# Edge keys by rows behind tile 2's ReLUs, and more warm transposes, in a graph attention layer

## The chip, the cores and the metric

The kernel runs on one core of one Trainium2 chip. The metric is the device time of one execution in microseconds (us). The time before is 299.84 us, the median of three runs (299.47 to 299.85).

## What is computed

The layer takes 384 nodes with 1024 features, a list of 6528 edges (`src`, `dst` and a type each), and weights. It normalises, applies a ReLU, projects twice to queries, keys and values for 16 heads of 64, adds a mask that is built from the edges, takes a softmax, multiplies by the values, projects once more and adds the input:

```
h = maximum(layernorm(x), 0)
q = h @ wq.T + bq;  k = h @ wk.T + bk;  v = h @ wv.T + bv
q2 = (q @ wiq.T + biq) by heads;  k2, v2 likewise
mask = full((N, N), -inf);  mask[src, dst] = softplus(edge_type_weights)[edge_type - 1]
mask's diagonal: softplus(w)[3] where still -inf
attn = softmax(q2 @ k2^T * scale + mask)
out = x + (attn @ v2) @ wo.T + bo
```

An edge can stand in the list more than once; the last one counts. So the kernel has to find, for each edge, whether the same (src, dst) cell comes again later.

## The kernel before, in words

All matrices are float32, and each product is made of three TensorE products: every operand is split into a high part in a reduced float32 format and the low rest, and high x high, high x low and low x high are added (`mm3`, lines 368 to 370).

The weights come as 56 chunks of 128 x 1024 (512 KB), in the order v, q, iv, k, then iq and ik in turn, then o. `load(w)` issues the DMA of chunk w on SP's queue into one of four `raw` buffers, so load(4) waits until chunk 0 has been read for the last time, load(5) for chunk 1, and so on. `split_hi(w)` (L77, ScalarE) and `split_lo(w)` (L82, VectorE or GpSimd) make the two parts. `slot_head(w)`, called ahead of each chunk's products, splits chunk w + 2, evacuates the products of the slot before, and issues load(w + 5).

The start, where the change lies, treats the three tiles of 128 nodes (t = 0, 1, 2) one after another:

- `ln_bn` (L247) and `ln_mean` (L250) take the mean and variance of a tile on VectorE.
- `ln_sub` subtracts the mean. For tiles 0 and 1, ScalarE does columns 0 to 511 (L276) and GpSimd the rest (L278); for tile 2 VectorE does both halves (L280).
- `ln_transpose` turns the tile with eight TensorE transposes (L288), four to a PSUM bank.
- `ln_hi` is the ReLU, which also makes the high part (L295 on ScalarE, L297 on VectorE, for the first half of tile 2). `ln_lo` (L302, VectorE) makes the low part.
- `ln_root`, `ln_rstd` and `ln_row` make the row of reciprocal deviations by which the projections are multiplied afterwards (`evac_row`, L389 to L391).
- `warm(n)` (L308) issues n transposes of the identity whose results nobody reads. `WARM` says how many stand ahead of tile 0's transposes, after them, and after tile 1's.

Chunk 0 is split by VectorE (L344) and GpSimd (L346) in two halves. The products of chunks 0 and 1 are issued in pieces (`pieces`, L380), in the order in which their operands become ready; from chunk 2 on a chunk is 24 products (L368 to L370).

The mask is prepared beside this. Each edge gets a key, 384 src + dst. `key_rows` computes the keys in another layout on VectorE (L180) and stores them in DRAM (`krow`, L181). `key_load(g, s)` (L201) reads a stretch of them back, broadcast to all 128 partitions; key_load(0, 0), (0, 1) and (0, 2) bring what the first 18 chunks of edges need. `mask_detect` (L213, VectorE) compares each chunk of edges with its row; the first three stand behind the evacuation of chunk 0's products, and all three key loads are needed for them. `mask_index` (L219, L220) makes the addresses, GpSimd scatters the values into three tables in DRAM (L224), which SP has cleared (`table_clear`, L145), and `mask_load` (L233) and `mask_select` (L237) bring them back well behind.

The order on every engine is the order in which the program is written: nothing is rescheduled. A DMA on SP's queue that waits holds up all those written after it. The small loads (`erows`, `edges`, `bcol`, `etw`) and chunks 0 and 1 are issued on SP right after the three tiles of x.

Of the kernel before, what the change touches and what calls it, by code (L numbers as in the profile page):

```python
# [14 lines left out]
N, D, NT, KT, NP = 384, 1024, 3, 8, 8  # L15
# [7 lines left out]
def gnn_kernel(ctx: ExitStack, tc: tile.TileContext, x, edges, erows, etw, wq, wk, wv, wiq, wik, wiv, wo,  # L23
# [6 lines left out]
    nc = tc.nc  # L30
# [8 lines left out]
    EB = 6  # L39
    NTAB, RNG = 3, EC // 3  # L40
    JI = [0, 1, 3, 5, 8, 11, 14, RNG]
    WARM = (20, 3, 0)

    def bank(tag):
        return psum.tile([128, 512], F32, tag=tag, name=tag, bufs={"g": 3, "a": 1}.get(tag, 2))
# [14 lines left out]
    def load(w):  # L60
        if w >= NCH:
            return
        n, m = chunks[w]
        raw[w] = wpool.tile([128, D], F32, tag="raw", name="raw", bufs=4)
        nc.sync.dma_start(raw[w], W[n][m])

    def split_hi(w, dst=None, dve=False):
        if w >= NCH:
            return
        if dst is None:  # L70
            t = wpool.tile([128, 2, D], F32R, tag="whl", name="whl", bufs=4)
            dst = (t[:, 0, :], t[:, 1, :])
        whl[w] = dst
        if dve:
            nc.vector.tensor_copy(dst[0], raw[w])
        else:
            nc.scalar.activation(dst[0], raw[w], AF.Copy)  # L77
# [51 lines left out]
    def mask_consts():  # L129
        nc.gpsimd.memset(upper, 1.0)  # L130
        nc.gpsimd.affine_select(upper, upper, pattern=[[1, 128]], compare_op=OP.is_gt, fill=0.0, base=0,
                                channel_multiplier=-1)
        nc.gpsimd.iota(dump.bitcast(I32), pattern=[[0, 1]], base=CELLS, channel_multiplier=1)
        nc.gpsimd.tensor_copy(w8[:, 8:9], dump.bitcast(I32))
        nc.gpsimd.memset(zero, 0.0)
# [42 lines left out]
    def key_rows():  # L178

        nc.vector.scalar_tensor_tensor(krt[:, :EC], er[:, :EC], float(N), er[:, EC:], op0=OP.mult, op1=OP.add)  # L180
        nc.sync.dma_start(krow.rearrange("c j -> (c j)").rearrange("(p e) -> p e", p=128), krt[:, :EC])  # L181
# [5 lines left out]
    def parts(g):  # L187
        return [(r * RNG + g * PA, min(r * RNG + (g + 1) * PA, (r + 1) * RNG)) for r in range(NTAB)]
# [3 lines left out]
    def key_load(g, s):  # L192

        if s == 0:
            t = work.tile([128, 2, NT, N], F32R, tag="pt", name="rows")
            krv[g] = t.bitcast(F32).rearrange("p a k n -> p (a k n)")
        c0, c1 = parts(g)[s]
        dst = krv[g][:, s * PA * 128:(s * PA + c1 - c0) * 128]
        for c in range(c0, c1):
            rows[c] = krv[g][:, (s * PA + c - c0) * 128:(s * PA + c - c0 + 1) * 128]  # L200
        nc.sync.dma_start(dst, krow[c0:c1, :].rearrange("c j -> (c j)").partition_broadcast(128))  # L201
# [44 lines left out]
    def ln_bn(t, h):  # L246
        nc.vector.bn_stats(lnt[:, 30 + 12 * t + 6 * h:36 + 12 * t + 6 * h], xt[t][:, h * 512:(h + 1) * 512])  # L247

    def ln_mean(t):
        nc.vector.bn_aggr(lnt[:, 2 * t:2 * t + 2],  # L250
                          lnt[:, 30 + 12 * t:42 + 12 * t].rearrange("p (a b) -> p a b", a=2))
        if t < 2:
            nc.scalar.mul(negm[:, t:t + 1], lnt[:, 2 * t:2 * t + 1], -1.0)

    def ln_root():
        nc.scalar.activation(root, var, AF.Sqrt, bias=epsc, scale=0.25)
        nc.scalar.activation(vq, var, AF.Identity, bias=epsc, scale=0.25)
# [15 lines left out]
    def ln_sub(t, c0, c1, eng):  # L273
        src, dst = xt[t][:, c0:c1], xn[t][:, c0:c1]
        if eng is nc.scalar:
            nc.scalar.activation(dst, src, AF.Identity, bias=negm[:, t:t + 1])  # L276
        elif eng is nc.gpsimd:
            nc.gpsimd.tensor_tensor(dst, src, lnt[:, 2 * t:2 * t + 1].to_broadcast([128, c1 - c0]), OP.subtract)  # L278
        else:
            nc.vector.tensor_scalar(dst, src, lnt[:, 2 * t:2 * t + 1], None, op0=OP.subtract)  # L280

    def ln_transpose(t):
        pss = []
        for half in range(2):
            ps = bank("st"[half] if t < 2 else "ga"[half])
            for j in range(4):
                k = half * 4 + j
                nc.tensor.transpose(ps[:, j * 128:(j + 1) * 128], xn[t][:, k * 128:(k + 1) * 128], ident)  # L288
            pss.append(ps)
        return pss  # L290

    def ln_hi(t, half, ps, eng=None):
        hi = hT[:, 0, half * 4:half * 4 + 4, t * 128:(t + 1) * 128]
        if eng is None:
            nc.scalar.activation(hi, ps.rearrange("p (k n) -> p k n", k=4), AF.Relu)  # L295
        else:
            eng.tensor_scalar(hi, ps.rearrange("p (k n) -> p k n", k=4), 0.0, None, op0=OP.max)  # L297
# [7 lines left out]
    def warm(n):  # L305
        for i in range(n):
            ps = bank("g")
            nc.tensor.transpose(ps[:, :128], ident, ident)  # L308

    mask_consts()  # L310
    warm(WARM[0])
    ln_bn(0, 0)
# [4 lines left out]
    p0 = ln_transpose(0)  # L317
    warm(WARM[1])
    ln_bn(1, 0)
# [6 lines left out]
    ln_bn(2, 0)  # L326
    ln_bn(2, 1)
    ln_mean(2)
    key_rows()
    load(2)  # L330
    load(3)
    for s in range(NTAB):
        key_load(0, s)
    ln_sub(2, 0, 512, nc.vector)
    ln_sub(2, 512, D, nc.vector)
    p1 = ln_transpose(1)
    warm(WARM[2])
    ln_hi(1, 0, p1[0])
# [8 lines left out]
    load(4)  # L347
    ln_hi(2, 0, p2[0], nc.vector)
    ln_hi(2, 1, p2[1])
    split_hi(1)  # L350
    ln_root()
    ln_lo(0, 0, p0[0])
# [533 lines left out]
```

## Time and profile before

| | |
|---|---|
| median of the three runs | 299.84 us |
| the profiled execution's own time | 298.95 us |
| its span, first to last instruction | 297.2 us |
| TensorE busy | 291.2 us, 98% of the span |
| VectorE, ScalarE, GpSimd busy | 202.4, 153.8, 155.7 us |
| first product of the projections | 10.16 us from the span's start |

The profile is that of one execution. PE is TensorE, PEld its loads of stationary operands, DVE VectorE, ACT ScalarE, POOL GpSimd, SP the engine whose queue issues most DMAs. A row of the timeline gives the start and the duration in us, the engine, the line of the code, the operation, what it writes and reads, its shape and how many were merged; in brackets stands the engine's idle time before it and what ended that. A merged row starts with the first of its instructions and ends with the last. TensorE's instructions overlap, so the time that each takes up is the distance from one start to the next, less than the duration shown. A row of the chain gives start, length and what was on the path that ended last.

### The profile page before, as it was taken

The page shows a single profiled execution, that of the slowest core. Times are in us where ns is not written, and L with a number is a line of the kernel's source. Part 1 is how long each engine was busy: PE and PEld are TensorE (multiplying, and loading weights), DVE is VectorE, ACT ScalarE, POOL GpSimd, SP SyncE. Part 2 cuts the span into 40 slices and gives each one's busy share as a digit, 9 for nine tenths or more (in the row PEclk, how much of TensorE's full clock was granted, in tenths as well). Part 3 has the DMA queues.
Part 4 walks back from the last instruction along what each step waited for, and adds up shares of the span by engine and source line. Part 5 has one row for each costly group of instructions (what it writes and reads, how often), then busy time and mean ns, then how long its engine had stood idle before and what let it go on. Part 6 is the DMA issues. An engine that isn't in the chain of part 4 may idle for free.

```text
span 297.2 us, 4982 instructions
## 1 busy us (share of the span) xinstructions
PE 291.2 (98%) x1654; PEld 276.5 (93%) x1654; DVE 202.4 (68%) x495; ACT 153.8 (52%) x288; POOL 155.7 (52%) x160
## 2 busy tenths in 40 slices
PE   6999999999999999999999999999999999999995
PEld 5999999999988889999999999999999998888884
DVE  4958977766856553888865676868686766696423
ACT  3784644433422222554336677778777767865310
POOL 3774567363857785710033656373746467976210
PEclk9999999999999999999999999999999999999999
DMA  7899864645396648393369784738374656900005
GB/s 279 277 324 398 292 207 131 225 143 212 116 303 202 197 153 289 113 342 112 117 167 261 206 216 115 202 93 223 99 221 121 170 144 176 348 10 0 2 3 209
DMA packets 22377, 55.12 MB, mean 185 GB/s; under 512 B 4816, under 2 KB 8400, under 8 KB 22352
## 3 DMA queue, kind: packets, MB, share of 16 engines
q1 hardware_dynamic: 19968, 52.42, 56.0%
q0 software_dynamic: 2064, 1.80, 2.1%
q10 hardware_dynamic: 320, 0.59, 0.9%
q8 instruction: 13, 0.21, 0.3%
q14 instruction: 12, 0.10, 0.1%
HBM read 40.39 MB, written 4.97 MB: 153 GB/s over the span
## 4 chain that ended last, share of the span: by engine, by line
PE 96%; DVE 1%; DMA 1%; ACT 0%; issue 0%
PE g L370 21%; PE g L368 21%; PE g L369 21%; PE a L758 6%; PE s L721 6%; PE t L741 5%; PE g L380 3%; PE s L369 2%; PE s L370 2%; PE s L368 2%; PE t L370 2%; PE t L369 2%; PE t L368 2%; DMA g<-in_x_dram 1%; DVE lnt L247 1%; PE a L369 1%
## 5 line engine op out<-in xcount | busy, mean ns | idle before, releaser
L368 PE MATMUL g<-g,whl 128*128 128x384 f32 x304 | 103.6, 341 | 0.0
L370 PE MATMUL g<-g,whl 128*128 128x384 f32 x304 | 101.8, 335 | 0.0
L369 PE MATMUL g<-g,whl 128*128 128x384 f32 x304 | 101.5, 334 | 0.0
L224 POOL DMA_INDIRECT tab<-val,idx x51 | 56.1, 1100 | 37.5 <-issue 11.0
L77 ACT ACTIVATE whl<-raw 128x1024 fp32r<-128x1024 f32 x51 | 53.6, 1051 | 29.7 <-PE g L370 21.1
L82 DVE TENSOR_TENSOR whl<-raw,whl 128x1024 fp32r<-128x1024 f32 x41 | 52.6, 1282 | 15.6 <-ACT whl L77 12.4
L736 POOL TENSOR_TENSOR e<-e,s 128x384 f32<-128x384 f32 x48 | 39.3, 829 | 43.1 <-DVE s L735 42.4
L369 PEld LDWEIGHTS g<-g,whl 128*128 128x128 f32 x304 | 57.2, 188 | 0.0
L368 PEld LDWEIGHTS g<-g,whl 128*128 128x128 f32 x304 | 57.1, 188 | 0.0
L370 PEld LDWEIGHTS g<-g,whl 128*128 128x128 f32 x304 | 57.0, 188 | 0.0
L82 POOL TENSOR_TENSOR whl<-raw,whl 128x1024 fp32r<-128x1024 f32 x11 | 26.4, 2398 | 30.8 <-ACT whl L77 28.1
L390 ACT ACTIVATE g<-f,bc 128x384 fp32r<-128x384 f32 x24 | 14.8, 618 | 52.7 <-DVE f L389 41.2
L751 DVE TENSOR_TENSOR pt<-t,pt 128x384 fp32r<-128x384 f32 x48 | 26.4, 549 | 15.3 <-ACT pt L750 15.0
L731 ACT ACTIVATE e<-e,s 128x384 f32<-128x384 f32 x48 | 29.2, 608 | 9.3 <-DVE s L727 8.1
L750 ACT ACTIVATE pt<-t 128x384 fp32r<-128x384 f32 x48 | 23.3, 486 | 13.6 <-PE t L741 13.3
L727 DVE CUSTOM_DVE_ANT_0 e<-s,ma 128x384 f32<-128x384 f32 x48 | 26.4, 549 | 3.6 <-PE s L721 3.4
L721 PE MATMUL s<-ks,qs 128*128 128x384 f32 x96 | 24.7, 338 | 0.0
L741 PE MATMUL t<-ident,e 128*128 128x128 f32 x144 | 23.5, 271 | 0.0
L389 DVE TENSOR_TENSOR f<-g,rrow 128x384 f32<-128x384 f32 x24 | 13.3, 556 | 13.9 <-PE g L370 13.7
L741 PEld LDWEIGHTS t<-ident,e 128*128 128x128 f32 x144 | 18.7, 140 | 3.1
L758 PE MATMUL a<-pt,vhl 128*128 128x384 f32 x96 | 20.8, 351 | 0.0
L721 PEld LDWEIGHTS s<-ks,qs 128*128 128x128 f32 x96 | 17.5, 188 | 0.8
(145 smaller groups left out, 416.2 us busy)
## 6 DMA issues: line engine op xcount, KB each, us to landing
ks<-nat SPq DMA_DIRECT2D x30, 192.0 KB
raw<-in_wv_dram SPq DMA_DIRECT2D x8, 512.0 KB
raw<-in_wq_dram SPq DMA_DIRECT2D x8, 512.0 KB
raw<-in_wiv_dram SPq DMA_DIRECT2D x8, 512.0 KB
raw<-in_wk_dram SPq DMA_DIRECT2D x8, 512.0 KB
raw<-in_wiq_dram SPq DMA_DIRECT2D x8, 512.0 KB
raw<-in_wik_dram SPq DMA_DIRECT2D x8, 512.0 KB
raw<-in_wo_dram SPq DMA_DIRECT2D x8, 512.0 KB
```

The source lines that it names most:

```text
L77: nc.scalar.activation(dst[0], raw[w], AF.Copy)
L82: (eng or nc.vector).tensor_tensor(lo, raw[w], hi.bitcast(F32), OP.subtract)
L224: nc.gpsimd.indirect_dma_start(out=tabs[c // RNG], out_offset=bass.IndirectOffsetOnAxis(ap=idx[:, c:c + 1], axis=0), in_=val[:, c:c + 1], ...
L368: nc.tensor.matmul(ps, lhi, rhi, start=first, stop=False)
L369: nc.tensor.matmul(ps, lhi, rlo, start=False, stop=False)
L370: nc.tensor.matmul(ps, llo, rhi, start=False, stop=last)
L721: nc.tensor.matmul(ps[:, :N], qs[:, o, t * 128:(t + 1) * 128], ks[:, o, s, :], start=(s == 0), stop=(s == 1))
L727: nc.vector.tensor_tensor_reduce(e, st_ps.pop(i)[:, :N], ma[:, t, :], -0.125, 3.0e38, OP.add, OP.min, s[:, 0:1])
L731: nc.scalar.activation(es[i], es[i], AF.Exp, bias=s[:, 0:1], scale=-1.0, accum_out=s[:, 1:2])
L736: nc.gpsimd.tensor_tensor(es[i], es[i], s[:, 2:3].to_broadcast([128, N]), OP.mult)
L741: nc.tensor.transpose(ps[:, k * 128:(k + 1) * 128], es[i][:, k * 128:(k + 1) * 128], ident)
L758: nc.tensor.matmul(ps[:, :N], vhl[:, k, p, 2 * o:2 * o + 2, :], pts[h][:, s, k, :], start=(k == 0 and s == 0), stop=(k == 2 and s == 1))
```

## The change

The step `key_rows`, with its store, and the three `key_load` calls of the first group move from ahead of tile 2's subtraction to behind the ReLUs of tile 2. They thereby come behind load(2), load(3) and load(4) on SP's queue, where they were ahead of load(2) (the store) and ahead of load(4) (the key loads). On VectorE the key instruction moves from between L250 and L280 to between L297 and the first L302. The warm transposes become 25 instead of 20 ahead of tile 0's, and 5 instead of 3 after them.

```diff
-    WARM = (20, 3, 0)
+    WARM = (25, 5, 0)
...
     ln_bn(2, 0)
     ln_bn(2, 1)
     ln_mean(2)
-    key_rows()
+    ln_sub(2, 0, 512, nc.vector)
+    ln_sub(2, 512, D, nc.vector)
     load(2)
     load(3)
-    for s in range(NTAB):
-        key_load(0, s)
-    ln_sub(2, 0, 512, nc.vector)
-    ln_sub(2, 512, D, nc.vector)
     p1 = ln_transpose(1)
     warm(WARM[2])
     ln_hi(1, 0, p1[0])
...
     load(4)
     ln_hi(2, 0, p2[0], nc.vector)
     ln_hi(2, 1, p2[1])
+    key_rows()
+    for s in range(NTAB):
+        key_load(0, s)
     split_hi(1)
     ln_root()
     ln_lo(0, 0, p0[0])
```

## The prediction

> **What bounds the kernel now.** I read the page first: engines' shares and the chain that ended last.
>
> ```profile
> PE 291.2 (98%) x1654; PEld 276.5 (93%) x1654; DVE 202.4 (68%) x495; ACT 153.8 (52%) x288; POOL 155.7 (52%) x160
> ...
> PE 96%; DVE 1%; DMA 1%; ACT 0%; issue 0%
> ```
>
> TensorE is the chain. So only two things can move the end: when its product stream begins, and a later stall in it. I then read the chain in order of time, from the span's start.
>
> ```profile
> 0.81 3.28 DMA g<-in_x_dram
> ...
> 5.66 1.30 DVE lnt L247 x2
> ...
> 6.98 0.22 DVE lnt L250
> ...
> 7.22 0.21 ACT lnt L253
> ...
> 7.46 0.73 ACT g L276
> ...
> 8.23 0.66 PE s L288 x4
> 8.89 0.45 PE t L288 x4
> 9.34 0.00 issue
> 9.34 0.63 PE g L288 x4
> 9.97 0.44 PE a L288 x4
> 10.41 8.16 PE g L380 x52
> ```
>
> The start is set by tile 1: its statistics on VectorE, its subtraction on ScalarE (ends 8.18), its transposes. Tile 2's transposes follow with no gap, and the products follow those. From 10.16 to the end TensorE shows no idle time. I compared each matmul's start with the one before: after 10.16 every step has its shape's usual length, but for some 0.05 us near 12.7, where it meets the end of GpSimd's low half (L346, 10.01 + 2.66 = 12.67).
>
> Third, the timeline by engine: VectorE, where the moved step is.
>
> ```profile
> 8.46 0.21 DVE L250 BATCH_NORM_AGGREGATE lnt<-lnt 128x2 f32<-128x12 f32 x1
> 8.59 0.16 DVE L180 SCALAR_TENSOR_TENSOR kr<-er 128x51 f32<-128x51 int32 x1
> 8.71 0.88 DVE L280 TENSOR_SCALAR g<-g,lnt 128x512 f32<-128x512 f32 x2
> ...
> 22.05 0.34 DVE L213 SCALAR_TENSOR_TENSOR junk<-rows,key,upper 128x128 bf16<-128x128 f32 x1
> ...
> 23.80 0.17 DVE L219 SCALAR_TENSOR_TENSOR ed<-cnt,key 128x3 f32<-128x3 f32 x1 [0.83 <-POOL val L174]
> ...
> 29.36 1.22 DVE L82 TENSOR_TENSOR whl<-raw,whl 128x1024 fp32r<-128x1024 f32 x1
> ```
>
> And SP's queue, which the diff reorders; each row is the issue, not the landing.
>
> ```profile
> 8.78 0.33 SPq L181 DMA_DIRECT2D krow<-kr  x1
> 9.15 0.91 SPq L65 DMA_DIRECT2D raw<-in_wv_dram  x2
> 10.69 1.29 SPq L201 DMA_DIRECT2D rows<-krow  x3
> 12.70 2.70 SPq L65 DMA_DIRECT2D raw<-in_wv_dram  x2
> ```
>
> **The change part by part.** *key_rows' VectorE instruction leaves its place before the subtraction.* It takes 0.16 us, but L280 reads the mean that L250 writes, and L250 ends at 8.46 + 0.21 = 8.67; L280 starts 0.04 later. That 0.04 is what any VectorE instruction waits for the result of the one before (L263 ends 15.31, L264 starts 15.35; L166 ends 18.13, L167 starts 18.17). L180 runs in that wait. Without it L280 still starts at 8.71. From above I bound the gain by the whole 0.16 us; it would need L280 to start before its operand is there, and tile 2's transposes are behind tile 1's until 9.33 anyway. I take 0.
>
> *It arrives after tile 2's first ReLU (L297), ahead of the low halves (L302).* Nearest row: the small instructions L156 and L157 start 0.11 and 0.08 apart from the next. So +0.1 us for the six L302, 0.07 to 0.16. The cover: the low halves of k 0 to 3 are complete at 12.65 and of k 4 to 7 at 14.45, and the products that read them begin at 14.94 and 15.63 (single matmuls of the timeline). That leaves over 1 us. Cost 0; without the cover, 0.1.
>
> *Warm transposes 20 to 25 and 3 to 5.* The 20 take 4.27 us from 1.43, a step of 0.213 at first and 0.109 from the 19th on (start 5.28). Five more end their turns near 5.5 + 5 x 0.109 = 6.05; tile 0's transposes start at 6.68, when ScalarE's subtraction is there. Two more after tile 0 start at 7.94 and 8.05 and are through at 8.16; tile 1 starts at 8.23. Both lie in idle time, by 0.6 and 0.07 us: cost 0. Their gain in this execution is 0 too, since the clock is already up.
>
> Here a rule speaks for another sum. The row first:
>
> ```profile
> L308 PE MATMUL g<-ident x23: 272/417/472, 1.4 to 7.8; 128*128 128x128 f32 x23
> ```
>
> 417 ns before the switch at 5.2, 272 after, and still 272 after the idle 0.98 us that follows. The Trainium skill, "TensorE: Matmul & The Clock Gate", Part 1 (the HAM clock gate), says that the clock rises after a busy window of about 3.4 us which runs freely, so that the moment differs from run to run. An estimate from that page: the switch could come between 1.43 + 3.4 = 4.8 and 8.3. If it is late and the idle 0.98 us spoils the window, the sixteen tile transposes cost 0.213 instead of 0.109, +1.7 us, and the first products more; longer warming would then save 1 us or so. By the row the sum is 0. Against it, in a late switch the 25 end at 1.43 + 25 x 0.213 = 6.76, later than 6.68, and two more cost 0.43: up to 0.4 us lost. I take the row: 0, from -1 to +0.4.
>
> *SP's queue.* load(2) and load(3) no longer stand behind the key store, which waits for L180 at 8.75. They follow the small loads (SP free at 5.42), held only by the landing signals they reuse (x tiles 1 and 2, landed 5.6 and 7.1 by the trace's signals). Their bytes then follow raw[1] and the biases, which end at 10.5, so load(2) lands near 10.5 + 1.3 = 11.8 instead of 13.8. ScalarE's split_hi(2) (now 13.85, idle 1.49 for that DMA) can follow L257 at 12.35, and the softplus behind it gains about 0.4, as it then waits for L157. Nothing on TensorE's path.
>
> The price: the key store and the three key loads now stand behind load(4), which waits for GpSimd to free raw[0] at 12.67 (issue 12.70). So the store is issued at 13.07 instead of 8.78. It needs 1.9 us alone (8.78 to the first key load's 10.69), but load(4)'s 512 KB are ahead of it; loads took from 3.6 us (a lone one later, 50.5 to 54.1) to 4.7 (load(2)) from issue to landing. Load(4) lands at 16.3 to 17.4, the store just after. The key loads follow at 16.4 to 17.5, their bytes 2 us later. The three took 15.1 to 20.5 = 5.4 us behind load(3); at the 0.121 us of most of their packets, 24 per engine, it would be 2.9. So the last lands between 16.4 + 2 + 2.9 = 21.3 and 17.5 + 2 + 5.4 = 24.9; I take 23.5, against 20.5.
>
> The first three mask_detects ran at 22.05, so VectorE now waits on the key rows. Behind it on VectorE stand mask_index, the evacuation of slot 1, the low half of w = 4, six more detects, the evacuation of slot 2 and the low half of w = 5 (29.36). VectorE is full from 24.14 to there, so a delay is handed on whole. Two detects can go before the last load; the third needs 0.35, and its accumulator read 0.08: mask_index at 23.5 + 0.5 = 24.0 instead of 23.80. Delay 0.2. Cover: slot 2 starts at 19.45 and a slot is 24 x 0.1733 = 4.16, so w = 4 is wanted at 27.77 (ready 25.83, slack 1.9) and w = 5 at 31.93 (ready 29.36 + 1.22 = 30.58, slack 1.35). Hence 0 on the end; without this cover 0.2. TensorE begins to lose when the last key load lands after 23.80 + 1.35 - 0.5 = 24.65.
>
> Weight loads 5 to 8 and table clears behind the key loads come some 1 to 2 us later. Slacks are from 2 us up (raw[5] had landed by 24.4 and its low half ran at 29.36). Cost 0; the bytes are the same. The masks are loaded by about 128 and selected at 147: nothing there.
>
> Sum: 0 + 0 + 0 + 0 against the profiled execution's 298.95 (span 297.2 and 1.75 around it). The median of the runs, 299.84, lies 0.9 above it; the difference of 0 is put on the median: 299.8.
>
> **The rivals.**
> *A, nothing moves* (0.67): 299.8, within 299.4 and 300.2, about the spread of the three runs. For it: three limits at the start, none of them touched. In it lies the rival that the change does what it says, and starts tile 2 earlier: at most 0.16 us, 299.7.
> *B, the clock* (0.16): in undisturbed runs the switch comes late, and the 0.9 us between median and profiled execution is the price of it; longer warming takes it away: 299.84 - 0.9 = 298.9. For it: 0.98 us of idle TensorE right after the switch, and the median's distance. Against: the runs' spread of 0.4 is small for a moving window, and the distance has other possible causes.
> *C, the key rows come late* (0.17, slower): one mechanism, VectorE waiting at the first detect, with w = 5 as the place where TensorE stops. From 24.65 on, each microsecond of lateness is one of time, since nothing later has idle time to give back. Landing at 25.7 gives 300.9; my upper bound of 24.9 alone costs 0.25, so it needs slower transfers than before, which rows as slow as theirs between 16 and 20 (228 ns and more for a packet) make possible.
>
> **How the numbers follow.** The likeliest is A, 299.8. 0.2% is 0.6 us, about what a measurement can tell from no change: A is the middle, B faster, C slower. The range takes A whole, B to 299.0 and C to 300.6.
>
> **What would show it.** After: L280 still at 8.71 and the products at 10.16; warm transposes of 25 and 5 ending before 6.7 and 8.2; SP's two weight loads before 8 and the key store after 13; the first detect at 21.5 to 24, with its idle time put to the key rows' DMA; no TensorE gap near 31.9. Wrong if the products start elsewhere, if the timed runs fall near 299.0 with the same trace (B), or if TensorE idles before slot 5 (C).

## The result and the profile after

The changed kernel takes 300.37 us (median of 21 runs, 299.34 to 300.87), against 299.77 (21 runs, 298.76 to 300.45) for the kernel before on the same chips: a ratio of 1.0022, 95% interval 1.0013 to 1.0031. It is slower by some 0.65 us. That is rival C, at a smaller price than the 300.9 us written there.

The profiled execution took 300.38, its span is 298.7. The page, engines' shares and chain that ended last:

```profile
PE 292.9 (98%) x1661; PEld 277.6 (93%) x1661; DVE 202.4 (68%) x495; ACT 153.8 (51%) x288; POOL 157.1 (53%) x160
...
PE 88%; DMA 6%; DVE 4%; SPq 1%; issue 0%; DVEq 0%
```

TensorE was 96% of the chain before and is 88% now. The chain in order of time (start, length, what) says where the rest lies: it does not go through the products at all until 33.58.

```profile
9.29 0.89 DVE g L280 x2
...
11.44 0.62 DVE kr L180
...
13.64 4.51 DMA krow<-kr
...
19.02 7.17 DMA rows<-krow
...
26.28 0.37 DVE junk L213 x2
...
27.64 1.13 DVE whl L82
...
32.39 1.14 DVE whl L82
33.53 0.04 issue
33.58 0.44 PE g L370
```

The reader can walk the price down: the store (issued at 13.64, landed after 4.51 us), the last key load (landed at 26.18), the third detect, two low halves, and only then a product that waits. Ahead of 13.64 the chain names VectorE's rows, but the key instruction was through at 12.06. What held the store was the load ahead of it on SP's queue: load(4) went out at 13.27, when GpSimd had freed raw[0] at 13.24. SP's queue in the timeline:

```profile
5.92 7.67 SPq L65 DMA_DIRECT2D raw<-in_wv_dram  x3
13.64 0.43 SPq L181 DMA_DIRECT2D krow<-kr  x1
18.17 1.28 SPq L201 DMA_DIRECT2D rows<-krow  x3
```

VectorE, with its idle time and the releaser in brackets:

```profile
11.35 0.71 DVE L180 SCALAR_TENSOR_TENSOR kr<-er 128x51 f32<-128x51 int32 x1
...
24.42 0.35 DVE L213 SCALAR_TENSOR_TENSOR junk<-rows,key,upper 128x128 bf16<-128x128 f32 x1 [1.67 <-DMA rows<-krow]
...
26.28 0.35 DVE L213 SCALAR_TENSOR_TENSOR junk<-rows,key,upper 128x128 bf16<-128x128 f32 x1 [1.50 <-DMA rows<-krow]
...
26.75 0.17 DVE L219 SCALAR_TENSOR_TENSOR ed<-cnt,key 128x3 f32<-128x3 f32 x1
```

And TensorE in slot 5, where the third product of a group (L370) is the one that needs the low half of w = 5:

```profile
32.94 0.34 PE L369 MATMUL g<-g,whl 128*128 128x384 f32 x1
33.58 0.44 PE L370 MATMUL g<-g,whl 128*128 128x384 f32 x1 [0.30 <-DVE whl L82]
```

From 32.94 to 33.58 is a step of 0.64 us where 0.17 is usual, and the next takes 0.28. Two steps at 28.5 to 29.1, in slot 4, are long in the same way, by 0.25 together.

The first product starts at 10.74, not 10.16. This is not the change: x's third tile landed at 7.70 here and at 7.12 in the profile before, and in the profiles of the twelve kernels below at 7.4 to 8.0, also where nothing ahead of it differs. VectorE's first instruction on that tile, before and after:

```profile
7.14 1.29 DVE L247 BATCH_NORM_STATS2 lnt<-g 128x6 f32<-128x512 f32 x2
```

```profile
7.72 1.29 DVE L247 BATCH_NORM_STATS2 lnt<-g 128x6 f32<-128x512 f32 x2 [0.60 <-DMA g<-in_x_dram]
```

From the landing to the first product it is 3.04 to 3.05 us in all fourteen profiles, that of the kernel before included. The profiled execution of the kernel before was an early one. So I use as a measure the time from the first product to TensorE's last instruction: 283.57 before, 284.43 after. The loss inside it is 0.86 in this profile.

### The profile page after: what moved, and what is told of

It is laid out like the page before. It is cut to its first block, busy times and chain, and to the rows that moved or that the text cites. A ratio compares the mean times of both kernels' runs of the same rounds, so it can differ in the third digit from the quotient of the medians.

```text
span 298.7 us, 4994 instructions
## 1 busy us (share of the span) xinstructions
PE 292.9 (98%) x1661; PEld 277.6 (93%) x1661; DVE 202.4 (68%) x495; ACT 153.8 (51%) x288; POOL 157.1 (53%) x160
## 4 chain that ended last, share of the span: by engine, by line
PE 88%; DMA 6%; DVE 4%; SPq 1%; issue 0%; DVEq 0%
PE g L370 20%; PE g L368 20%; PE g L369 20%; PE a L758 6%; PE s L721 6%; PE t L741 5%; DMA rows<-krow 2%; DMA g<-in_x_dram 2%; PE s L369 2%; PE s L370 2%; PE s L368 2%; PE t L370 2%; PE t L369 2%; PE t L368 2%; DMA krow<-kr 2%; DVE whl L82 1%
## 5 line engine op out<-in xcount | busy, mean ns | idle before, releaser
L370 PE MATMUL g<-g,whl 128*128 128x384 f32 x304 | 102.0, 336 | 0.3 <-DVE whl L82 0.3
L224 POOL DMA_INDIRECT tab<-val,idx x51 | 57.3, 1124 | 38.7 <-DMA tab<-val,idx 15.4
L82 DVE TENSOR_TENSOR whl<-raw,whl 128x1024 fp32r<-128x1024 f32 x41 | 52.6, 1284 | 16.3 <-ACT whl L77 16.3
L370 PEld LDWEIGHTS g<-g,whl 128*128 128x128 f32 x304 | 57.1, 188 | 0.9 <-DVE whl L82 0.9
L82 POOL TENSOR_TENSOR whl<-raw,whl 128x1024 fp32r<-128x1024 f32 x11 | 26.4, 2400 | 30.3 <-ACT whl L77 27.6
L751 DVE TENSOR_TENSOR pt<-t,pt 128x384 fp32r<-128x384 f32 x48 | 26.4, 549 | 15.3 <-ACT pt L750 15.0
L750 ACT ACTIVATE pt<-t 128x384 fp32r<-128x384 f32 x48 | 23.3, 486 | 13.6 <-PE t L741 13.3
L741 PE MATMUL t<-ident,e 128*128 128x128 f32 x144 | 23.5, 271 | 0.0
L389 DVE TENSOR_TENSOR f<-g,rrow 128x384 f32<-128x384 f32 x24 | 13.3, 555 | 11.8 <-PE g L370 11.8
L213 DVE SCALAR_TENSOR_TENSOR junk<-rows,key,upper 128x128 bf16<-128x128 f32 x51 | 16.3, 354 | 3.2 <-DMA rows<-krow 3.2
```

Source lines behind the costliest of these rows:

```text
L82: (eng or nc.vector).tensor_tensor(lo, raw[w], hi.bitcast(F32), OP.subtract)
L224: nc.gpsimd.indirect_dma_start(out=tabs[c // RNG], out_offset=bass.IndirectOffsetOnAxis(ap=idx[:, c:c + 1], axis=0), in_=val[:, c:c + 1], ...
L370: nc.tensor.matmul(ps, llo, rhi, start=False, stop=last)
L741: nc.tensor.transpose(ps[:, k * 128:(k + 1) * 128], es[i][:, k * 128:(k + 1) * 128], ident)
```

## The experiments

Every kernel was timed against the kernel before on the same chip; ratios carry their 95% intervals. "First to end" is the measure above; "loss" is its excess over 283.57. The edits are cuts of the programs, with "..." for what lies between.

**The two parts apart.** Only the warm transposes:

```diff
-    WARM = (20, 3, 0)
+    WARM = (25, 5, 0)
```

> Only the warm transposes change (25 and 5 instead of 20 and 3); the keys stay ahead of tile 2's subtraction. Theory K (the added time is TensorE waiting in slots 4 and 5 because the key rows land late, behind load(4)): no such wait here, 299.8 us, within 0.3 of before. Rival W (more warm transposes push tile 0's and tile 1's transposes back when the clock rises late, or change the clock): slower by 0.4 to 0.6. Rival X (the early weight loads delay x's third tile, and with it the first product): no early loads here, so as before, 299.8.

299.62 us, ratio 0.9988 (0.9977 to 1.0000); no wait in slots 4 and 5, first to end 283.59. The warm transposes alone cost nothing, and if they gain, it is 0.1%. Rival W falls. This profile's chain also shows who sets the start when x's third tile is late:

```profile
1.72 5.95 DMA g<-in_x_dram
...
9.02 0.21 DVE lnt L250
9.23 0.08 DVE kr L180
9.30 0.46 DVE g L280
9.76 0.14 issue
9.90 0.63 PE g L288 x4
```

Here L180 stands ahead of L280, and on the chain. But L280 starts 0.035 us after L250's end (9.227 to 9.262), as it does without L180 (0.036, 9.249 to 9.285, in the changed kernel). In all fourteen profiles it is 0.035 to 0.037.

Only the move (the changed kernel with `WARM = (20, 3, 0)`):

> Only the move of the keys, warm transposes 20 and 3 as before. Theory K: all of the loss, so 300.3 to 300.6, first detects waiting for the key rows until 25 to 26 and TensorE idle ahead of the low product of slot 5. Rival W: 299.8, as before. Rival X: 300.3 to 300.6 too, with the first product at about 10.7 instead of 10.2.

299.90 us, ratio 1.0004 (0.9994 to 1.0015). Theory K had expected the whole loss here; the move alone has none that can be measured. Its SP queue and its third detect:

```profile
13.76 0.43 SPq L181 DMA_DIRECT2D krow<-kr  x1
17.00 1.28 SPq L201 DMA_DIRECT2D rows<-krow  x3
```

```profile
24.95 0.35 DVE L213 SCALAR_TENSOR_TENSOR junk<-rows,key,upper 128x128 bf16<-128x128 f32 x1 [1.22 <-DMA rows<-krow]
```

VectorE waits here too, but the store landed after 3.2 us instead of 4.5 and the last key load at 24.85 instead of 26.18, and TensorE has no long step: first to end 283.53.

Only the early weight loads (`load(2)` and `load(3)` ahead of the store, the store and the key loads still ahead of load(4)):

```diff
     key_rows()
     load(2)
     load(3)
+    key_store()
     for s in range(NTAB):
         key_load(0, s)
```

(`key_store` is key_rows' DMA, cut off from its VectorE instruction.)

> load(2) and load(3) are issued ahead of the key store, as in the change, but the key instruction stays ahead of tile 2's subtraction and the store and the key loads stay ahead of load(4). Warm transposes as before. Theory K: key rows land by 21 to 22, no wait of TensorE, 299.8. Rival X: x's third tile lands at 7.7 instead of 7.1, first product near 10.7, 300.3 to 300.5.

299.69 us, ratio 1.0004 (0.9989 to 1.0019), last key load 22.17, first to end 283.57. x's third tile landed at 7.62, as it did at 7.67 in the warm-only kernel, which has no early loads. Rival X falls.

SP's order of the change, the key instruction in its old place on VectorE:

```diff
     key_rows()
     load(2)
     load(3)
-    for s in range(NTAB):
-        key_load(0, s)
...
     ln_hi(2, 1, p2[1])
+    key_store()
+    for s in range(NTAB):
+        key_load(0, s)
```

> SP's queue in the order of the change (load(2), load(3), load(4), store, key loads), but the key instruction on VectorE stays ahead of tile 2's subtraction; warm transposes as before. Theory K: the whole loss, as in the move alone: last key load lands near 25 to 26, TensorE waits 0.3 to 0.8 us in slots 4 and 5, 300.3 to 300.6. If VectorE's own shift (the key instruction took 0.71 us in its new place) is a part of the loss, this one is faster than the move alone by 0.3 or more.

299.82 us, ratio 1.0007 (0.9994 to 1.0019), store 13.60 to 16.62, last key load 24.39, no loss, where K had again expected all of it. So the warm transposes, the move, the early loads and SP's new order each cost nothing alone.

**Together, apart again, and the dose.** The changed kernel once more:

> The changed kernel once more, for a second profile and a fresh comparison on one chip with the three beside it. Theory K, now with an edge (the last key load lands at 24.4 to 26.2 from run to run, and TensorE loses only what is over 25.2): 299.9 to 300.5, with the loss in the profile equal to the landing less 25.2. Rival F (a 16 KB read of instructions, at 15.9 in the changed kernel's first profile, holds one DMA engine for 0.9 us just ahead of the key store's last packets, and that is the difference from the move alone): such a read again between 15.5 and 17 and the store landing after 17.5. Rival W (the warm transposes themselves): slower than the move again by 0.4, without a wait in slots 4 and 5.

300.56 us, ratio 1.0024 (1.0010 to 1.0038); store 13.53 to 18.08, last key load 26.04, first to end 284.36. It repeats. The move alone once more, on the same chip:

> The move alone once more, warm transposes 20 and 3, beside the changed kernel. Theory K with an edge: the same as the changed kernel within 0.3, since the key loads are as late. Rival F or W: faster than the changed kernel by 0.3 to 0.6, as in the first comparison.

299.69 us, ratio 0.9998 (0.9987 to 1.0010); store 13.96 to 17.15, last key load 24.80, first to end 283.58. It repeats too. What differs between the two ahead of the store's landing? The DMA records from 15 to 17.2 us (queue, packets, MB, share), first of the changed kernel, then of the first move-alone kernel:

```profile
DMA packets 243, 0.38 MB, mean 172 GB/s; under 512 B 160, under 2 KB 160, under 8 KB 242
...
q1 hardware_dynamic: 242, 0.36, 47.2%
q8 instruction: 1, 0.02, 2.6%
```

```profile
DMA packets 252, 0.40 MB, mean 183 GB/s; under 512 B 160, under 2 KB 160, under 8 KB 252
...
q1 hardware_dynamic: 252, 0.40, 51.2%
```

The one packet on q8 is a 16 KB read of instructions that takes 0.9 us on one DMA engine. It starts at 15.87 in the changed kernel and at 15.99 in its second profile, at 19.4 and 19.6 in the move alone. The store is 128 packets, so eight for each of 16 engines if they are shared out evenly. In the changed kernel the last eight run alone, from the end of the read (16.77) to 17.02; in the move alone all have ended by 16.56. The store's landing is told by sixteen signals. In the changed kernel fifteen are in by 16.86 and the last comes at 18.15; in the move alone all come between 16.50 and 16.99.

The first three detects moved behind the low half of w = 4, in the changed kernel:

```diff
-        detects((0, 3, 6)[s] if s < 3 else 2)
+        detects((0, 0, 9)[s] if s < 3 else 2)
```

> The changed kernel with the first three detects moved from slot 1 to slot 2, where nine then stand in place of six. VectorE so meets the key rows only behind the evacuation of slot 1 and the low half of w = 4. Theory K: the key rows are then there when the first detect comes (28 or so), no wait for them and none of TensorE in slots 4 and 5: 299.6 to 299.9. Rival W: still 300.3.

299.71 us, ratio 0.9990 (0.9977 to 1.0002). The key rows are as late as ever (store 13.96 to 18.49, last load 26.30), but no detect waits:

```profile
24.43 1.23 DVE L82 TENSOR_TENSOR whl<-raw,whl 128x1024 fp32r<-128x1024 f32 x1 [1.17 <-ACT whl L77]
26.63 0.34 DVE L213 SCALAR_TENSOR_TENSOR junk<-rows,key,upper 128x128 bf16<-128x128 f32 x1
```

w = 4's low half is made at 24.43 instead of 27.55, and first to end is 283.55. This settles the path of the loss: lateness costs only through VectorE standing at the first detects.

Key instruction, store and key loads behind load(5), again in the changed kernel:

```diff
     ln_hi(2, 1, p2[1])
-    key_rows()
-    for s in range(NTAB):
-        key_load(0, s)
...
         load(w + 5)
+        if w == 0:
+            key_rows()
+            for s in range(NTAB):
+                key_load(0, s)
```

> The changed kernel with the key instruction, its store and the key loads one weight load further back, behind load(5). Theory K as a dose: the last key load lands near 28.3 and every microsecond over 25.2 is one of time, so TensorE loses 2.5 to 3.5 us in slots 4 and 5 and the time is 302.2 to 303.2. If lateness of the key rows is given back somewhere later, or is not what counts: under 301.

301.00 us, ratio 1.0045 (1.0029 to 1.0061), loss in the profile 1.25. The sign is as expected; the size (302.2 to 303.2) and the landing were not: 26.78, not 28.3. The store went out at 17.93, when load(4) was all but in (18.10) and load(5), issued at 15.9, well on its way (19.37); it landed right behind that, at 19.60.

**Which part of the combination.** Store ahead, key loads alone behind load(4), warm transposes 25 and 5; the edit against the kernel before:

```diff
-    WARM = (20, 3, 0)
+    WARM = (25, 5, 0)
...
     key_rows()
+    key_store()
     load(2)
     load(3)
-    for s in range(NTAB):
-        key_load(0, s)
...
     ln_hi(2, 1, p2[1])
+    for s in range(NTAB):
+        key_load(0, s)
```

> Warm transposes 25 and 5; the key instruction and its store stay ahead (the store ahead of load(2)), and only the three key loads go behind load(4). Theory K with the store's round trip as the long part: the store has landed by 12, the key loads are issued at 13.6 instead of 18.1 and the last lands near 22, before 25.2: no wait of TensorE, 299.5 to 299.9, whatever the instruction read does. Rival W (warm transposes together with late loads): 300.3.

299.58 us, ratio 0.9999 (0.9986 to 1.0011), with the key loads issued at 13.40 and the last landed at 22.49, although the instruction read came at 15.5 here. So the store's place behind load(4) is needed for the loss.

The changed kernel with the key instruction in its old place on VectorE (the SP order of the change, warm transposes 25 and 5):

> The changed kernel with the key instruction back in its old place on VectorE, store and key loads still behind load(4), warm transposes 25 and 5. Theory F (the 16 KB instruction read meets load(4) and the store): if the read falls between 15.5 and 16.5 and the store lands after 17.5, 300.2 to 300.6; if the store lands before 17.2, 299.6 to 299.9. If VectorE's 0.6 us at the new place is a needed part of the loss: 299.7 with the store landing late all the same.

300.51 us, ratio 1.0029 (1.0014 to 1.0043). Read at 16.3, store 13.83 to 18.38, last key load 26.11, loss 0.59. Beside the same kernel with 20 and 3, without a loss (1.0007, 0.9994 to 1.0019), this says that VectorE's shift is not needed, and that the warm transposes are.

25 and 3, and 20 and 5, in the move:

```diff
-    WARM = (25, 5, 0)
+    WARM = (25, 3, 0)
```

> The move with 25 warm transposes ahead and 3 after (five more than the move alone, ten TensorE instructions). Theory F: the read comes early (15.5 to 16.5), the store lands at 18 or later, and TensorE loses 0.7 to 0.9: 300.3. If the count isn't enough to bring the read forward: read after 19, store at 17, 299.8.

```diff
-    WARM = (25, 5, 0)
+    WARM = (20, 5, 0)
```

> The move with 20 warm transposes ahead and 5 after (two more than the move alone, four TensorE instructions). Theory F: the read stays after 19 or comes early; the store's landing and the time must go with it: 17.0 and 299.8, or 18 and 300.3. A loss with the store at 17.0, or none with the store at 18.1, speaks against F.

With 20 and 5: 299.52 us, ratio 1.0002 (0.9989 to 1.0015), read at 19.2, store landed 16.56, last key load 24.45, no loss, as theory F (the instruction read meets load(4) and the store) has it. With 25 and 3 the profile has the whole loss (read at 16.3, store 13.89 to 18.41, last key load 26.29, loss 0.71, that execution's time 300.48), but the runs do not: median 299.52, ratio 0.9997 (0.9985 to 1.0008), with the profiled execution the slowest of all. Its executions seem to fall on either side; the profile of one can't say how often, and this stays open.

**All profiles together.** The loss obeys one line:

```
kernel                first     last key      landing less   loss
                      product   load landed   first product
before                10.16     20.50         10.34          0
warm only             10.72     21.42         10.70          0
early loads           10.66     22.17         11.51          0
store ahead           10.44     22.49         12.05          0
queue only            10.70     24.39         13.69          0
move again            11.05     24.80         13.75          0
move only             10.87     24.85         13.98          0
move, 20 and 5        10.46     24.45         13.99          0
old place, 25 and 5   10.93     26.11         15.18          0.59
move, 25 and 3        10.99     26.29         15.30          0.71
after, again          10.63     26.04         15.41          0.79
after                 10.74     26.18         15.44          0.86
behind load(5)        11.01     26.78         15.77          1.25
```

In the five with a loss, landing less first product less loss is 14.59, 14.59, 14.62, 14.58 and 14.52, in the table's order: the edge, beyond which each microsecond is one of time. The eight others lie under it. Only the kernel with later detects (landing less first product 15.24, no loss) has another edge, as it should.

## Why the prediction went wrong, step by step

**The start, right in the sum, wrong in the path.** L280 does not start earlier without L180, the warm transposes cost nothing, the products start no sooner. But I named tile 1 as what sets the start, as the chain does. Tile 2 sets it: the first product came 3.04 to 3.05 us after the landing of x's third tile in every profile, with 7.12 and 10.16 in the one that I read. The landing moves from run to run, and it explains most of the 0.9 us between profile and median that I had given to the clock in rival B. Rival B gets at most 0.1%, by the warm-only kernel. The clock rose at 4.3 to 6.8 us over the fourteen profiles, in part earlier than my estimate of 4.8 to 8.3. In the changed kernel's profile it rose at 6.77, with all 25 transposes begun, and the products still began 3.04 us after the tile's landing.

**The early weight loads, mis-sized without harm.** load(2) landed at 13.42, not near 11.8, though it was issued at 5.92; before it was 13.82. Nothing on TensorE's path hung on it.

**VectorE's shift, mis-sized without harm.** The key instruction took 0.71 us and put the low halves back by 0.63, not by 0.1. The kernel with the key instruction in its old place loses as well.

**The failing step: the landing of the last key load.** I put it at 23.5, at most 24.9, and so the delay's cost on TensorE at 0; the landing was 26.18. Of that, 0.58 is the later start, which moves the edge as well. Counted from the first product I had 13.3, at most 14.7; it was 15.4. Two terms of the sum are wrong:

- The three key loads, 2 + 2.9 to 5.4 us from their issue, took 8.0, and 7.6 to 8.0 in all nine kernels with the store behind load(4). I had counted the 5.4 from load(3)'s landing at 15.1. By the trace's DMA records their packets had begun at 13.77 and ended at 20.17, so they took 6.4 us before the change too (6.7 after it, 19.12 to 25.82); 0.121 us was the time of about half of them, not of most.
- The store's landing, "just after" load(4), I had at 6.2 to 7.3 us after the first product. It came at 5.9 to 6.1 in the four of these nine kernels in which no instruction read fell among the store's packets, and at 7.4 to 7.5 in the other five, the changed kernel among them.

With the key loads at their measured length, my own range for the store would have put the last landing at 13.9 to 15.3 after the first product, on both sides of the edge: a cost of 0 to 0.8 us, not 0. Where in that range the changed kernel falls is decided by the store. The instruction read, which seems to hold it up, stood nowhere in my sum: I had costed the added transposes as time on TensorE alone.

**The edge and the way, right, the edge's closeness partly luck.** 24.65 against a first product at 10.16 is 14.49; measured 14.52 to 14.62. Two small errors offset each other: the wait begins at the third product of a group, 0.35 us later than I counted, while the steps from the landing to that product, and the long step after it, cost some 0.2 more. The wait at the first detects, w = 5 as the main place (the two long steps at w = 4 are 0.25 of the 0.86) and the price of one to one beyond the edge are as rival C had them. It should have had a larger chance: its point of decision lay inside my own bounds for the landing, and a landing assembled from three waits one behind another deserved a wider upper bound.

Shown: that the late store is needed (store ahead, no loss), that the detects' place is needed (later detects, no loss), and that the warm transposes and the late store are needed together (each alone, no loss). Not shown by an edit of its own: that the instruction read is what delays the store. For it: it stood at 15.8 to 16.4 in each profile in which the store landed after 18; in four of the five with the store at 18.1 to 18.5, the store's last eight packets began within 0.02 us of the read's end; and in all five at least fourteen of the sixteen signals were in by 17.3, and the last came at 18.1 to 18.5. The queue-only kernel had the read at 16.2 without harm, its last store packet ending at that moment.

Open is what sets the moment of the read. In the move it goes with the number of warm transposes (19.4 and 19.6 with 20 and 3, 19.2 with 20 and 5, 16.3 with 25 and 3, 15.9 and 16.0 with 25 and 5). But with the key instruction in its old place it was 16.2 with 20 and 3 and 16.3 with 25 and 5, and only the second lost. So how the warm transposes add to the loss is not settled. Open too is why the store's last signal came 0.8 to 1.1 us after its last packet in the five; it was 0.4 to 0.5 in the other four with the store behind load(4), but 0.8 to 1.1 also in three kernels with the store ahead of the loads and no read near it (before, warm only, store ahead).

No version beats the kernel before beyond its interval; the warm transposes alone and the later detects are nearest (0.9988 and 0.9990).

## What to carry to other kernels

A step moved back on an in-order queue is to be costed to the landing of the last transfer that depends on it, each hop with the traffic ahead of it and its bytes timed from their first packet to their last, and then compared with the slack as a range: if the edge lies in the range, the change is a risk, not a zero. Use the slack from the event that sets the clock of the stage (here landing less first product), so that one execution's luck drops out. And before believing one profile's start, look at it in a second: a chain that names one of two paths of nearly equal length says little about the other.

## What the hardware showed beyond that

- A small VectorE instruction took 0.71 us instead of 0.16 while GpSimd ran an elementwise instruction beside it (L180 at 11.35, beside L343 from 10.58 to 13.24); L262 took 0.41 in the profile before, beside GpSimd's L82, and 0.16 after, when GpSimd was between L149 and L152. That GpSimd is the cause was not tested.
- The 384 packets of 3 KB of the first three key loads took 5.5 to 6.7 us from first to last in the fourteen profiles. Before, half of them took 0.125 us or less, after, one in seven. What slows them is open.
- The step per warm transpose fell from 0.213 to 0.109 us when the trace's clock record began at full speed: at 5.22 us before, at 6.77 after, at 4.3 to 6.8 over the fourteen profiles, with the first transpose at 1.43 in each. So the moment moves from run to run, as the Trainium skill says ("TensorE: Matmul & The Clock Gate", Part 1), but by 2.5 us here, against the 0.5 either way that the page gives. The first product followed x's third tile by 3.04 to 3.05 us all the same.
